# The feed-forward part's low-rank inputs moved from TensorE to a redundant weight row and to VectorE

## The chip, the cores and the metric

The kernel runs on one core of one Trainium2 chip. The core has a matrix engine (TensorE, PE in the profile, with its weight loads as PEld), three engines for elementwise work (VectorE or DVE, ScalarE or ACT, GpSimd or POOL), and SyncE (SP), which here issues most of the DMAs. Each engine works through its own queue in order; semaphores tie them together. The metric is the device time of one launch in microseconds. A smaller number is better.

## The reference

Input x has 8 sequences of 256 rows of 512. Every row is normalized, xn = (x - mean) / sqrt(var + 1e-5). Two branches start from xn:

```python
# feed-forward branch; each weight is a quarter, repeated four times, plus a rank-2 term
def linear(x, wq, A, B):
    return x @ tile(wq, (1, 4)).T + (x @ A.T @ B.T) * 0.5
h = silu(linear(xn, w1q, a1, b1)) * linear(xn, w3q, a3, b3)    # 1376 wide
g = silu(linear(h, w2q, a2, b2))                               # 512 wide
# attention branch, 128 heads: s = attention(xn), with latent q, k, v and a 64-wide rope part
out = x + s * g
```

A weight that is its quarter repeated four times needs only the sum of the four quarters of xn: xs = xn[0:128] + xn[128:256] + xn[256:384] + xn[384:512], and x @ tile(wq).T = xs @ wq.T, a contraction over 128 instead of 512. The rank-2 term has two numbers per row of x and branch (x @ a1.T, x @ a3.T) and is added on top.

The mean of each row of xn is zero, so the 128 numbers of xs sum to zero: one of them follows from the other 127. This is the redundancy that the change speaks of.

## The kernel before

The rows are taken in four blocks (`tb`) of 512. `first_phase` runs the whole feed-forward branch for all four blocks and stores its gates to DRAM; then the attention loop runs over 64 pairs of sequence and head group. Nothing is left to a planner: the order in which the code issues instructions is the order on each engine's queue. SyncE issues nearly all DMAs, in code order, and a DMA that must wait holds up those behind it.

One block on TensorE:

- `turn(tb)`: 16 transposes of the normalized x (the 128x512 tiles `xt`) into four PSUM banks; ScalarE and VectorE copy them to `act1`, feature-major. VectorE and GpSimd then add up the four quarters (`xs`, lines 429 to 431).
- `narrow(tb)`: the product `pm` of xn with `ck_sb`, which holds both low-rank inputs and the rope key; VectorE scales it into `mid` (line 446). Rows 0, 1 and 32, 33 of each half of `mid` are the low-rank numbers (already times 0.5). The rope rows go to DRAM (`krs_d`).
- `down(tb)`: the product `pp` with attention's down weights (`cs_d` in DRAM), and `sum_x`, which stores sums and differences of quarters for attention (`xs_d`), four of them computed on GpSimd (line 157).
- Six steps `u`, each for two of the eleven chunks of 128 hidden features (the last step has one). `low(tb, u)` multiplies the two low-rank numbers of each row with `b13_sb`, contraction 2, into fresh PSUM banks `px` and `py` (line 473). `main(tb, u)` adds the main product of `xs` with `w1_sb` and `w3_sb` on top (line 172, by `on_columns`, four matmuls of 32 columns side by side). ScalarE takes the silu of `px` (line 488), VectorE multiplies it with `py` into `hT` (line 490; in the last three chunks, whose 88 + 32 rows belong to different quarters, in two narrow instructions, lines 493 and 494).
- `fold` (GpSimd, lines 508 to 510) sums the quarters of `hT` into `h4`, `low_out` (line 520) makes the second layer's low-rank numbers, which line 530 and line 532 put into rows 96 and 97 of the last part of `h4`: the second layer already carries its low-rank term as two more rows of its weight.
- `gate_out`: the product `pf` over `h4`, the last silu, and four stores to `gates_d`.

The blocks overlap by hand: `norm(tb + 1)` (VectorE's statistics, GpSimd's Newton steps for the reciprocal root) stands after step 1 of block `tb`, the normalization itself (ScalarE, line 410) after step 4, `turn(tb + 1)`, `narrow` and `down` between the six steps and `gate_out(tb)`. `load_x` runs one to two blocks ahead. In the last block attention's own preparation (`between(2)` to `between(7)`: sums of rope weights, `Prepare`, `values`, `Project`) stands between the steps. `between(0)` is `set_up`: it loads and rearranges attention's up and value weights, mostly on GpSimd (lines 602 to 623), right after `narrow(0)`.

PSUM has eight banks, all from one pool. A step takes four; the tags `gate` and `hT` have two buffers each, `act1` one, `xt` six. At the start 48 transposes of the identity into a bank that nobody reads keep TensorE occupied while the first x arrives.

Of the kernel before, what the change touches and what calls it, by code (L numbers as in the profile page):

```python
# [9 lines left out]
F32 = mybir.dt.float32  # L10
# [6 lines left out]
P = 128  # L17
# [20 lines left out]
def mla_ffn_gate_kernel(  # L38
# [42 lines left out]
    cs_d = [dram.tile([P, TB], F32, name=f"cs_d{n}") for n in range(NTB)]  # L81
    krs_d = [dram.tile([R, TB], F32, name=f"kr_d{n}") for n in range(NTB)]
# [221 lines left out]
    def first_phase(between):  # L304
# [8 lines left out]
        b13_sb = fw.tile([98, NCH, P], F32, name="b13_sb")  # L313
# [4 lines left out]
        xts, xns, xnT, xsum, mids = {}, {}, {}, {}, {}  # L318
# [8 lines left out]
        def load_chunks(to, of):  # L327

            of = of.rearrange("p (q f) -> p q f", q=4)
            nc.sync.dma_start(  # L330
                out=to[:, 0:8].rearrange("p (q n) m -> p q (n m)", q=4), in_=of[:, :, 0:256]
            )
            nc.sync.dma_start(out=to[:, 8:11, 0:88], in_=of[:, 0:3, 256:344])
            nc.sync.dma_start(
                out=to[:, 8:10, 96:128],
                in_=of[:, 3, 256:320].rearrange("p (m i) -> p m i", m=2),
            )
            nc.sync.dma_start(out=to[:, 10, 96:120], in_=of[:, 3, 320:344])

        for t in (w1_sb, w3_sb, b13_sb):  # L340
            nc.gpsimd.memset(t[:, 8:11, 88:96], 0.0)
            nc.gpsimd.memset(t[:, 10, 120:128], 0.0)
# [17 lines left out]
        nc.sync.dma_start(out=wdn_sb, in_=w_down.rearrange("(c p) m -> p c m", p=P))  # L360
        for n in range(2):
            for k in range(2):
                load_chunks(
                    b13_sb[64 * n + 32 * k : 64 * n + 32 * k + 2], b13[32 * k : 32 * k + 2, :]
                )
        load_chunks(w1_sb, w1t)
        load_chunks(w3_sb, w3t)
        load_x(1)

        def norm(tb):  # L370


            mv = f2.tile([P, 4, 2], F32, tag="mv", name=f"mv_{tb}")
            for n in range(4):
                s6 = f2.tile([P, 6], F32, tag="st", name=f"st_{tb}_{n}")
                nc.vector.bn_stats(s6, xts[tb][n])
                nc.vector.bn_aggr(mv[:, n, :], s6)
# [21 lines left out]
            off = f2.tile([P, 4], F32, tag="off", name=f"off_{tb}")  # L399
            if tb:  # L400
                nc.gpsimd.tensor_mul(off, mv[:, :, 0], r)
                nc.gpsimd.tensor_scalar(off, off, -1.0, None, ALU.mult)
            return mv, r, off

        def norm_rest(tb, mv, rstd, off):
            xns[tb] = xts[tb]
            for n, xn in enumerate(xts[tb]):
                one = rstd[:, n : n + 1]
                if tb:
                    nc.scalar.activation(xn, xn, AF.Identity, bias=off[:, n : n + 1], scale=one)  # L410
                else:
                    nc.vector.tensor_scalar(xn, xn, mv[:, n, 0:1], one, ALU.subtract, ALU.mult)

        def turn(tb):
            a = f1.tile([P, KT, TB], F32, tag="act1", name=f"act1_{tb}")
            xnT[tb] = a
            for n in range(4):
# [4 lines left out]
                if n % 2 == 0:  # L422
# [4 lines left out]
            xs = f2.tile([P, TB], F32, tag="xs", name=f"xs_{tb}")  # L427
            xs2 = f1.tile([P, TB], F32, tag="tmp", name=f"xs2_{tb}")
            nc.vector.tensor_add(xs, a[:, 0, :], a[:, 1, :])
            nc.gpsimd.tensor_add(xs2, a[:, 2, :], a[:, 3, :])  # L430
            nc.vector.tensor_add(xs, xs, xs2)
            xsum[tb] = xs

        def over_xn(tb, name, weights):
            ps = bank(f"{name}_{tb}")
            for cols in (ds(0, S), ds(S, S)) if name == "pm" and tb == 0 else (ds(0, TB),):
# [6 lines left out]
        def narrow(tb):  # L443
# [3 lines left out]
            mids[tb] = mid  # L447
# [11 lines left out]
        sets, hTs, h4s, mid2ps = {}, {}, {}, {}  # L459
# [6 lines left out]
        def low(tb, u):  # L466

            sets[tb, u] = []
            for i, c in enumerate(pair(u)):
                for k in range(2):  # L470
                    ps = bank(f"p{'xy'[k]}_{tb}_{u}_{i}")
                    r = slice(64 * i + 32 * k, 64 * i + 32 * k + 2)
                    nc.tensor.matmul(  # L473
                        ps, b13_sb[r, c], mids[tb][r], start=True, stop=False, skip_group_check=True
                    )
                    sets[tb, u].append(ps)

        def main(tb, u):
            n = u // 2
# [3 lines left out]
            for i, c in enumerate(pair(u)):  # L483
                px, py = sets[tb, u][2 * i : 2 * i + 2]
                on_columns(px, w1_sb[:, c], xsum[tb], False, True)
                on_columns(py, w3_sb[:, c], xsum[tb], False, True)
                gate = f2.tile([P, TB], F32, tag="gate", name=f"gate_{tb}_{u}_{i}")
                nc.scalar.activation(gate, px, AF.Silu)
                if c < 8:
                    nc.vector.tensor_mul(h[:, c // 2, :], gate, py)  # L490
                else:
# [4 lines left out]
                    )  # L496

# [52 lines left out]
        idle = bank("idle")  # L550
        for n in range(48):
            nc.tensor.transpose(idle[:, ds(n % 4 * P, P)], ident, ident)
        norm_rest(0, *norm(0))
        turn(0)
        narrow(0)
        between(0)
        for to, of in ((a2_sb, a2), (w2_sb, w2t), (w2_sb[96:98, 2, :], b2[0:2, :])):
            nc.sync.dma_start(out=to, in_=of)
        down(0)
        for tb in range(NTB):  # L560
            more = tb + 1 < NTB
            for u in range(6):
                low(tb, u)
# [4 lines left out]
                if u == 1 and more:  # L568
                    stats = norm(tb + 1)
# [407 lines left out]
```

## Time and profile before

| | |
|---|---|
| median of three runs | 2009.84 us (2007.26 to 2011.14) |
| profiled execution | 2012.79 us, span 2011.0 us |
| granted TensorE clock, mean | 0.998 |
| busy: TensorE / VectorE / ScalarE / GpSimd | 1998.9 / 1522.8 / 1079.4 / 725.9 us |
| first product of block 0, 1, 2, 3 (line 473) | 21.73, 70.99, 122.48, 170.70 us |
| first attention score (line 688) | 238.43 us |

A line of the groups reads: line of the kernel, engine, operation, output and inputs by name, shapes, how often, then busy microseconds and the mean length of one in nanoseconds, then the idle time of the engine just before them and what ended it. A line of the timeline reads: start, length, engine, line, operation, operands, how many instructions are merged. On TensorE each float32 matmul shows as two records, and records that overlap are each shown at full length, so that the distance from start to start is the price, not the length. The chain of waits is followed back from the last instruction and says which engine each part of the span hung on.

### The profile page before, as it was taken

How to read it: one execution, taken by the hardware profiler on the slowest of the kernel's cores; microseconds unless marked ns; L12 is line 12 of the kernel's file. 1: busy time of each engine (PE TensorE's matmuls, PEld its weight loads, DVE VectorE, ACT ScalarE, POOL GpSimd, SP SyncE). 2: the span in 40 equal slices, each digit the busy share in tenths (PEclk: the TensorE clock that was granted, in tenths of full speed). 3: DMA queues.
4: the chain of work that ended last, by engine and by line, in shares of the span. 5: the costliest groups of instructions: out<-in, count | busy, mean ns of one | idle time of the engine just before them, and what ended most of it. 6: DMA issues, size and time to landing. Idle time of an engine off the chain costs nothing.

```text
span 2011.0 us, 86602 instructions
## 1 busy us (share of the span) xinstructions
PE 1998.9 (99%) x38112; PEld 1412.7 (70%) x38112; DVE 1522.8 (76%) x2601; ACT 1079.4 (54%) x2958; POOL 725.9 (36%) x1076
## 2 busy tenths in 40 slices
PE   9999999999999999999999999999999999999998
PEld 4334577777777777777777767777777767777776
DVE  4332387878788777878787877878787877888788
ACT  2222365565556554555655645565565555556654
POOL 5445545545552323233233233223323323232231
PEclk9999999999999999999999999999999999999999
DMA  5233322222223223222223233222223222222212
GB/s 169 87 113 135 113 95 84 68 87 86 86 82 123 80 91 112 91 87 78 74 86 123 66 112 105 84 81 86 81 92 102 90 93 81 86 86 72 80 55 70
DMA packets 118188, 184.78 MB, mean 92 GB/s; under 512 B 10450, under 2 KB 84082, under 8 KB 117812
## 3 DMA queue, kind: packets, MB, share of 16 engines
q1 hardware_dynamic: 117812, 179.23, 26.4%
q8 instruction: 302, 4.95, 1.0%
q14 instruction: 74, 0.61, 0.1%
HBM read 145.12 MB, written 34.08 MB: 89 GB/s over the span
## 4 chain that ended last, share of the span: by engine, by line
PE 97%; DVE 2%; issue 0%; DMA 0%; ACT 0%; POOL 0%; SPq 0%; DVEq 0%
PE q L172 39%; PE sc L688 34%; PE av L734 11%; PE po L172 2%; PE pf L172 2%; PE px L172 2%; PE py L172 2%; PE px L473 1%; PE pm L172 1%; PE qq L250 1%; PE vps L285 1%; PE pp L172 1%; DVE pt L717 1%; DVE nmx L701 0%; PE pm L520 0%; PE xpt L420 0%
## 5 line engine op out<-in xcount | busy, mean ns | idle before, releaser
L707 ACT ACTIVATE pr<-sc,nmx 128x256 f32<-128x256 f32 x2048 | 816.5, 502 | 473.8 <-DVE nmx L701 471.0
L701 DVE TENSOR_REDUCE nmx<-sc 128x2 f32<-128x512 f32 x1024 | 635.6, 683 | 291.3 <-PE sc L688 267.4
L717 DVE STREAM_TRANSPOSE pt<-pr 128x512 f32<-128x512 f32 x1024 | 635.2, 678 | 0.0
L172 PE MATMUL q<-x,ws 128*32 128x256 f32 x8192 | 488.9, 379 | 0.6 <-POOL ws L136 0.6
L688 PE MATMUL sc<-act,qr 32*128 32x256 f32 x8192 | 489.0, 374 | 0.0
L215 POOL TENSOR_TENSOR e<-e,e 128x256 f32<-128x256 f32 x128 | 93.8, 733 | 1057.5 <-ACT e L210 570.6
L688 PEld LDWEIGHTS sc<-act,qr 32*128 32x128 f32 x8192 | 421.2, 185 | 22.2 <-issue 0.2
L172 PEld LDWEIGHTS q<-x,ws 128*32 128x32 f32 x8192 | 265.7, 110 | 177.2 <-POOL ws L136 1.1
L172 PE MATMUL q<-x,w 128*32 128x256 f32 x6144 | 381.5, 381 | 0.2 <-DMA w<-in_w_rope_dram 0.2
L172 PEld LDWEIGHTS q<-x,w 128*32 128x32 f32 x6144 | 186.9, 110 | 155.0 <-ACT pr L707 35.4
L688 PE MATMUL sc<-kc,qcm 32*128 32x256 f32 x4096 | 281.2, 387 | 0.0
L734 PE MATMUL av<-pt,vpad 128*32 128x128 f32 x8192 | 236.4, 273 | 1.9 <-ACT pr L707 1.2
L734 PEld LDWEIGHTS av<-pt,vpad 128*32 128x32 f32 x8192 | 226.3, 110 | 14.5 <-issue 3.0
L688 PEld LDWEIGHTS sc<-kc,qcm 32*128 32x128 f32 x4096 | 198.4, 184 | 52.1 <-issue 40.1
L210 ACT COPY e<-q 128x256 f32<-128x256 f32 x512 | 204.1, 399 | 27.9 <-PE q L172 26.3
L754 ACT ACTIVATE acc<-av,sides_sb 128x256 f32<-128x256 f32 (+1 forms) x130 | 54.3, 470 | 245.9 <-PE av L734 245.9
L270 POOL TENSOR_TENSOR qcm<-qc,mask_sb 128x1024 f32<-128x1024 f32 x64 | 122.3, 1911 | 9.6 <-ACT qc L260 9.6
L217 POOL TENSOR_TENSOR qr<-e,e 128x256 f32<-128x256 f32 x128 | 93.7, 732 | 10.0
L216 POOL TENSOR_TENSOR e<-e,e 128x256 f32<-128x256 f32 x128 | 93.5, 731 | 10.0
L227 DVE TENSOR_TENSOR qr<-e,q 128x256 f32<-128x256 f32 x128 | 53.9, 421 | 43.4 <-POOL e L215 24.4
L300 POOL COPY vpad<-vall 32x128 f32<-32x128 f32 x256 | 74.9, 293 | 14.8 <-ACT vall L292 4.4
L490 DVE TENSOR_TENSOR hT<-gate,py 128x512 f32<-128x512 f32 x32 | 21.5, 687 | 73.9 <-PE py L172 47.4
(105 smaller groups left out, 1107.4 us busy)
## 6 DMA issues: line engine op xcount, KB each, us to landing
w<-in_w_rope_dram SPq DMA_DIRECT2D x128, 512.0 KB
ws<-sums_d SPq DMA_DIRECT2D x96, 512.0 KB
sums_d<-ws SPq DMA_DIRECT2D x32, 512.0 KB
x<-xs_d SPq DMA_DIRECT2D x28, 256.0 KB
xt<-in_x_dram SPq DMA_DIRECT2D x16, 256.0 KB
xs_d<-xt SPq DMA_DIRECT2D x16, 256.0 KB
gate_d<-gs SPq DMA_DIRECT2D x16, 256.0 KB
g<-gate_d SPq DMA_DIRECT2D x16, 256.0 KB
```

Of the source, the lines that this page charges most:

```text
L172: nc.tensor.matmul(to[tile_], w[:, tile_], x, start=start, stop=stop, skip_group_check=True)
L210: nc.scalar.copy(self.e[i], self.banks[i])
L215: nc.gpsimd.tensor_add(m6, m6, m1)
L216: nc.gpsimd.tensor_add(m7, m7, m6)
L217: nc.gpsimd.tensor_add(self.out(1, 1), self.split(m7), self.split(m5))
L270: nc.gpsimd.tensor_mul(qcm, qks[b, sg // 2][0].rearrange("p (q i) -> p q i", i=32).unsqueeze(2).to_broadcast([P, 8, 4, 32]), mask_sb[:, ds ...
L300: nc.gpsimd.tensor_copy(vpad[rows, :, :, 8 * t + 4 * (sg % 2) :][..., :4], valls[b][rows, :, sg])
L688: nc.tensor.matmul(sc[r][:, h, :], lhs.rearrange("p t i -> p (t i)"), rhs, start=(part == 0 and h == 0), stop=(part == 2), skip_group_chec ...
L701: nc.vector.tensor_reduce(nmx[:, r, :], scs[n, f][r], AX.X, ALU.max, negate=True)
L707: nc.scalar.activation(p[:, h, :], scs[n, f][r][:, h, :], AF.Exp, bias=nmxs[n, f][:, r, h : h + 1])
L717: nc.vector.transpose(pts[n, f // 2, r].rearrange("p k q i -> p q k i")[:, ds(2 * (f % 2), 2)], prs.pop((n, f, r)).rearrange("p h (k j) -> ...
L734: nc.tensor.matmul(av[32 * r : 32 * r + 32, ds(half * P, P)], vpad[:, k, r, :], pt[r][:, k].rearrange("p q i -> p (q i)"), start=(k == 0), ...
```

## The change

The low-rank input term leaves TensorE. `low` and `b13_sb` go, and `main` starts its own PSUM groups. In their place:

- Each branch has two low-rank numbers per row of x. One of them is put into row 0 of the quarter sums, in place of the number that is there, so that the main product carries it. There are now two copies of the sums, `xs0` for the first weight and `xs1` for the second, and ScalarE writes row 0 of each from `mid`. Since the true row 0 is minus the sum of the other 127, the weight's first row is subtracted from all the others, and row 0 becomes the `b13` row: `less_first` and `rest_less_first`, whose subtrahend `firsts` is made by ten matmuls of contraction 2 from `others` and `rows` and copied out by ScalarE.
- The other number is added by VectorE: `lows` holds it broadcast over all partitions (written to DRAM as `low_d` and read back with a broadcast), `bcol_sb` has the matching `b13` column per chunk, and a scalar-tensor-tensor computes `lows * bcol + px` into the gate buffer, and the same for `py`, into `hT` or back into its PSUM bank.
- The silu now works in place on the gate buffer. Of the products gate times up, six per block go to GpSimd (in block 0 three, from step 2 on), the rest stay on VectorE.
- The order changes: loads of `w1`, `w3` before `b13`; 16 idle transposes instead of 48; `norm` one block earlier from block 2 on, after `gate_out`; the normalization spread over steps 0 to 3; `turn(tb + 1)` after step 4 with all four copies on ScalarE; the quarter sums in a function of their own (`sums`); `fold` and `low_out` after steps 3 and 5; attention's raw weights loaded in `between(-1)`, their rearrangement (`set_up`) after `gate_out(0)`.

```diff
-        b13_sb = fw.tile([98, NCH, P], F32, name="b13_sb")
+        bcol_sb = fw.tile([P, 16, 2], F32, name="bcol_sb")
...
+        rows = f1.tile([P, 3 * TB], F32, tag="h4", name="rows")[:, 0:F]
+        nc.scalar.dma_start(out=rows[64:97:32], in_=b13[0:33:32, :])
+        for k, wt in enumerate((w1t, w3t)):
+            nc.scalar.dma_start(out=rows[65 + 32 * k : 66 + 32 * k], in_=wt[0:1, :])
...
+        others = f2.tile([P, TB], F32, tag="gate", name="others")[:, 0:P]
+        nc.gpsimd.memset(others[64:128], 1.0)
+        nc.gpsimd.memset(others[64:128, 0:1], 0.0)
+        for k in range(2):
+            nc.gpsimd.memset(others[64 + 32 * k : 65 + 32 * k], 0.0)
+            nc.gpsimd.memset(others[64 + 32 * k : 65 + 32 * k, 0:1], -1.0)
...
-        for n in range(2):
-            for k in range(2):
-                load_chunks(
-                    b13_sb[64 * n + 32 * k : 64 * n + 32 * k + 2], b13[32 * k : 32 * k + 2, :]
-                )
-        load_chunks(w1_sb, w1t)
-        load_chunks(w3_sb, w3t)
+        for w_sb, wt in ((w1_sb, w1t), (w3_sb, w3t)):
+            load_chunks(nc.sync, w_sb, wt)
...
+        def sums(tb):
+            a = xnT[tb]
+            xs = [f1.tile([P, TB], F32, tag=f"xs{k}", name=f"xs{k}_{tb}") for k in range(2)]
+            xs2 = f1.tile([P, TB], F32, tag="tmp", name=f"xs2_{tb}")
+            nc.vector.tensor_add(xs[0], a[:, 0, :], a[:, 1, :])
+            nc.gpsimd.tensor_add(xs2, a[:, 2, :], a[:, 3, :])
+            nc.vector.tensor_add(xs[0], xs[0], xs2)
+            nc.scalar.copy(xs[1], xs[0])
+            xsum[tb] = xs
...
+            nc.sync.dma_start(out=low_d[tb], in_=mid[1:34:32, :])
+            lows[tb] = []
+            for k in range(2):
+                t = f1.tile([P, TB], F32, tag=f"low{k}", name=f"low{k}_{tb}")
+                nc.sync.dma_start(out=t, in_=low_d[tb][k : k + 1, :].to_broadcast([P, TB]))
+                lows[tb].append(t)
+                nc.scalar.copy(xsum[tb][k][0:1], mid[32 * k : 32 * k + 1])
...
+            for i, c in enumerate(chunks):
+                px, py = (bank(f"p{'xy'[k]}_{tb}_{u}_{i}") for k in range(2))
+                on_columns(px, w1_sb[:, c], xsum[tb][0], True, True)
+                on_columns(py, w3_sb[:, c], xsum[tb][1], True, True)
+                gates.append(f2.tile([P, TB], F32, tag="gate", name=f"gate_{tb}_{u}_{i}"))
+                ups.append((py, h[:, c // 2, :] if c < 8 and (tb or u > 1) and (i == 0 or u in (0, 2)) else py))
+                nc.vector.scalar_tensor_tensor(
+                    gates[i], lows[tb][0], bcol_sb[:, place(c), 0:1], px, ALU.mult, ALU.add
+                )
+                nc.scalar.activation(gates[i], gates[i], AF.Silu)
+                nc.vector.scalar_tensor_tensor(
+                    ups[i][1], lows[tb][1], bcol_sb[:, place(c), 1:2], py, ALU.mult, ALU.add
+                )
...
+                elif up is py:
+                    nc.vector.tensor_mul(h[:, c // 2, :], gate, py)
+                else:
+                    nc.gpsimd.tensor_mul(up, gate, up)
...
+        def less_first(k, engine):
+            w_sb = (w1_sb, w3_sb)[k]
+            for c in (0, 4):
+                engine.memset(w_sb[0:1, c : c + 4], 0.0)
+                one = w_sb[:, c : c + 4]
+                engine.tensor_sub(one, one, firsts[k][:, c : c + 4])
...
         for tb in range(NTB):
             more = tb + 1 < NTB
             for u in range(6):
-                low(tb, u)
                 main(tb, u)
-                if u in (2, 4):
+                if u in (3, 5):
                     fold(tb, u // 2 - 1)
                     low_out(tb, u // 2 - 1)
-                if u == 1 and more:
-                    stats = norm(tb + 1)
+                if u == 1 and tb == 0:
+                    stats = norm(1)
+                if more:
+                    for n in range(4):
+                        if u == (n if tb else 2 + n // 2):
+                            norm_one(tb + 1, n, *stats)
                 if u == 4 and more:
-                    norm_rest(tb + 1, *stats)
+                    turn(tb + 1)
...
             if more:
-                turn(tb + 1)
+                sums(tb + 1)
+                narrow(tb + 1)
                 low_out(tb, 2)
-                narrow(tb + 1)
                 down(tb + 1)
             else:
                 low_out(tb, 2)
             gate_out(tb)
+            if tb == 0:
+                between(0)
+            if tb + 2 < NTB:
+                stats = norm(tb + 2)
```

## The prediction

> **What bounds the kernel now.** I read the page first (engines and the chain that ended last), then the groups of the first 270 us with shapes apart, then TensorE's timeline and the stages as windows, last the clock.
>
> ```profile
> PE 1998.9 (99%) x38112; PEld 1412.7 (70%) x38112; DVE 1522.8 (76%) x2601; ACT 1079.4 (54%) x2958; POOL 725.9 (36%) x1076
> ...
> PE 97%; DVE 2%; issue 0%; DMA 0%; ACT 0%; POOL 0%; SPq 0%; DVEq 0%
> ```
>
> TensorE is 97% of the chain. A TensorE instruction that goes away shortens the run by its length, as long as what feeds and empties TensorE keeps up. That second half is what must be worked out.
>
> ```profile
> L473 PE MATMUL py<-mid,b_sb 2*128 2x512 f32 x88 | 28.4, 640 | 0.0
> ...
> L490 DVE TENSOR_TENSOR hT<-gate,py 128x512 f32<-128x512 f32 x32 | 21.5, 687 | 73.9 <-PE py L172 47.4 <-ACT gate L488 26.4
> ...
> L508 POOL TENSOR_TENSOR h<-hT 128x512 f32<-128x512 f32 x8 | 10.5, 1308 | 0.1
> ...
> L532 DVE SCALAR_TENSOR_TENSOR h<-pm,h 32x512 f32<-32x512 f32 x12 | 8.3, 691 | 1.4 <-ACT h L530 1.0
> ...
> L431 DVE TENSOR_TENSOR xs<-xs,xs 128x512 f32<-128x512 f32 x4 | 6.0, 1490 | 11.0 <-POOL xs L430 11.0
> ...
> L446 DVE TENSOR_SCALAR mid<-pm,cks_sb 128x512 f32<-128x512 f32 x4 | 3.0, 752 | 0.4 <-PE pm L172 0.3
> ```
>
> Line 473 is the low-rank input product, and VectorE's product at line 490 spends its time waiting. One step `u` of the timeline, block 2:
>
> ```profile
> 127.12 0.69 PE L473 MATMUL px<-mid,b_sb 2*128 2x512 f32 x1
> ...
> 128.19 1.07 PE L172 MATMUL px<-xs,w_sb 128*32 128x512 f32 x8
> ...
> 131.76 0.69 PE L473 MATMUL px<-mid,b_sb 2*128 2x512 f32 x1
> ```
>
> Start to start the step is 4.64 us; the four products in it follow each other at 0.86 (128.19, 129.07, 129.93, 130.79) and make 3.43, so `low` takes 1.21. The stages (blocks 0, 1, 2, then 3):
>
> ```profile
> 23.00:71.00 48.00, 47.63 (x413) 15.39 (x406) 19.56 (x34) 13.68 (x22) 34.54 (x67) 1.00 0.41 138
> 71.00:122.50 51.50, 51.38 (x428) 16.45 (x424) 19.49 (x33) 13.90 (x23) 21.89 (x29) 0.97 0.31 106
> 122.50:170.70 48.20, 48.08 (x424) 15.52 (x421) 19.59 (x33) 14.01 (x23) 27.57 (x37) 1.00 0.31 102
> 170.70:240.00 69.30, 69.30 (x980) 31.13 (x980) 14.98 (x25) 20.77 (x44) 35.18 (x43) 1.00 0.33 111
> ```
>
> Columns: stretch, length, busy of TensorE, its weight loads, VectorE, ScalarE, GpSimd, granted clock, DMA share, GB/s. VectorE has 19.5 of 48 us to do, room that the change fills. Block 1 is 3.3 us longer than block 2: ScalarE's gate stores waited up to 6 us for their buffer (line 547's transfers), TensorE ran dry for PSUM, and the clock fell:
>
> ```profile
> 79.00:80.00 1.00, 1.00 (x12) 0.72 0.70 266
> 80.00:81.00 1.00, 1.00 (x8) 0.50 0.61 221
> ```
>
> **Removed from TensorE.** 24 steps `low` by 1.21 us: 29.0 us, all on the path. Without it a block that keeps up is 22 products by 0.86 (18.9), `low_out` 2.8, `turn` 1.9, `pm` 3.43, `pp` 3.43, `pf` 10.44: 40.9 us against 48.2.
>
> **Added to VectorE.** Per block 22 scalar-tensor-tensor, each reading a broadcast row in SBUF, a column and a PSUM bank. No row shows this form. Line 532 (691, no column) bounds it below and line 431 above (mean 1490, 1754 in the three runs beside a reading GpSimd, 692 in the one without; two SBUF operands). I take 0.75, from line 446 (752), which has the column and the PSUM read. It also stands for the half that writes back into PSUM, of which there is no row. Products left on VectorE from block 1: two plus six of the narrow chunks, 8 by 0.69. Sum 16.5 + 5.5 = 22.0 us in the window in which TensorE does main, `low_out` and `turn`, 22.5. It fits by half a microsecond, with `pm`'s 3.43 as reserve before `low_out` 2 needs the last product.
>
> **Two gate buffers, GpSimd's products.** Six products per block go to GpSimd, 1.3 each (line 508). A gate buffer is free only after its product, so the next step's first VectorE operation waits for GpSimd: 0.75 + 0.75 + 1.31 = 2.8 us of a step's 3.43. Steady state holds. It breaks where GpSimd is busy with other things.
>
> **Block 0.** Three things are late here. (a) `lows` go through DRAM: `mid` ends at 19.2, the write and two 256 KB reads follow. The first x tile, on idle queues, took 2.8 us from issue (0.73 to 3.54); line 123's rope weights took 4.1 (195.35 to 199.43). Two such trips: 6 to 8.5 us; I take 6.0, the queues being near empty once the weights are in, so 25.2. TensorE does not stop; it has two steps of banks. (b) VectorE then does 8 operations and 4 products, 8.75 us (33.95), and only then `norm(1)`, 3.8 us (32.40 to 36.2 on the trace): 37.75. (c) GpSimd's 14 small steps, 4.0 us (41.51 to 45.39): 41.8. Two queues stand behind that. On ScalarE the normalizations of x for block 1 wait for it, and the later gates wait behind them. On GpSimd the two products of step 2 wait for it (first one done at 43.1), and they hold both gate buffers, so VectorE starts step 3 only at 43.1 and ends it, its product included, at 46.8 (four by 0.75 and 0.69). In step 4 VectorE frees the second gate's bank at 49.05, ScalarE's gate ends at 49.65, and `turn(1)`'s four copies, now all on ScalarE and behind that gate, end at 52.0 (four by 0.59). Its first two narrow products free the bank that step 5 lacks at 51.2 (46.8 + 3.0 + 1.4). From there TensorE is the bound again: step 5's second half, `low_out` 1, `pm`, `low_out` 2, `pp` and `pf` (0.86, 0.86, 3.43, 1.07, 3.43, 10.44) end at 71.3, against 71.0 now. So block 0 gives its 7.25 us back: +0.3. Bounds: trip of 2.8 us less, -3; of 8.5, +3, and 3 more if the clock falls (below).
>
> **Start-up.** 32 idle transposes go (4.6 us of the 6.9); ten products that copy the first rows come in: four 512 wide at 0.86 and six short, 4.6 us, and their ten copies on ScalarE, 4 us (0.59 for 512). TensorE has 8.25 to 11.17 and the freed time, ScalarE is idle to 12.32. Cover gone (rows landing after 7 us): up to 4 later. Three new DMAs stand on ScalarE's queue. On SP, 16 small `b13` loads go, two weight parts and six small loads come; the weights move from 12.4 to about 4.2, `x` for block 1 with them. Subtractions: GpSimd two by 1.28 and two fills by 0.53 after 17.44, first half ready at 19.3; VectorE's two after `mid`, 0.69 to 1.75 each, first half by 21.5; both before use at 21.7 and 22.6. The remaining chunks are due 17 us later. ScalarE's row copies (0.59 each) end at 20.4. Sum 0, bounds -1 and +4.
>
> **Block 1.** It loses the old 3.3 us only in part: SP waits out `low_d`'s write and issues two reads, some 2.8 us ahead of `kr_d`, `cs_d`, seven `xs_d` and the gate stores. By the same positions the first gate store is issued at about 71.5, as now, but TensorE needs the third bank 5.15 us after `pf` either way, so up to 1 us. `set_up` (27.48 to 36.4 on the trace, 8.9 us of GpSimd) now stands after `gate_out(0)`, with `norm(2)` behind it: GpSimd is free 6.5 us into block 1, its products are 4 us late, and through the gates VectorE is late by 3.5; TensorE's banks take most, 2 reach step 5. 40.9 + 2 + 0.6 = 43.5: -8.0 (bounds -11 and -4).
>
> **Blocks 2 and 3.** Block 2: 7.25 less 0.5 for the gates: -6.7. In block 3 attention's projections lie between the steps, VectorE has time, and GpSimd's two `sum_w` (5.9 us) stand before step 1's product: 2 us late, covered by values and Project. -6.7. Bounds -7.25 and -3 each. Attention, from 240 us on, is unchanged.
>
> Sum: 0 + 0.3 - 8.0 - 6.7 - 6.7 = -21.1. The profiled execution is 2012.79 (span 2011.0 and 1.8 around it), 2.95 above the median of 2009.84; from the median: **1988.7**.
>
> **A rule against it.** After the poor stretch 76 to 79 the trace shows half clock for some 3 us; block 0 will have TensorE idle about 43 to 47. The Trainium skill, "TensorE: Matmul & The Clock Gate", Part 1, has the clock halved after an idle window of about 3.4 us and whole after as much work. By that rule block 0 would come out some 2 us later, total about -19; the row at 80.00 agrees with a drop of that length. I kept 3 us in block 0's bound.
>
> **Rivals.** (1) Everything keeps up: `lows` early, no idle: 29 us and block 1's 3.3: -27 to -32, 1980. For it: GpSimd and ScalarE are under 60%. Against: the chain in block 0. (2) Half: VectorE at 0.85 with latencies between the engines costs 22 by 0.1 plus a step per block, some 3 us in four blocks, -10, 2000. For it: margin of 0.5 us in 22.5. (3) **Slower**, by one mechanism: the new operation, with row and column both in SBUF, is held up by GpSimd as line 431 is. At 1.75 VectorE has 22 us more per block, less 3.4 of reserve, less 7.25: +11.4, in three blocks +34, 2044. It decides at (7.25 + 3.4)/22 = 0.48 more, 1.23 us each. Against: lines 493 and 494 took 0.68 with GpSimd's line 508 running at 96.9; line 446 with its column 0.751 at 112.2, beside line 157. The Trainium skill, "SBUF — State Buffer", section "Who interferes with whom", says that a VectorE instruction with two SBUF inputs contends with a reading GpSimd, one with at most one does not; counting the column as an input would make it this rival. Line 446's row shows no such cost for a column, so the chance stays small. (4) Nothing is left: every term at its bad bound, +4 at the start, +6 in block 0, -4, -3 and -3 after it, sums to 0: within 0.2%, about 2010.
>
> **Chances.** Forecast (-16 to -26) 0.50; (1) 0.12; (2) (-5 to -16) 0.22; (4) 0.05; (3) 0.11. A fifth of a per cent, 4 us, is about what can be told from no change. Faster 0.84, same 0.05, slower 0.11. The forecast with (2) and most of (1): 1981 to 2004; the forecast's own 1984 to 1994.
>
> **What would show it.** Line 473 gone; blocks 1 and 2 near 43.5 and 41.5 us; block 0 about 48 with VectorE waiting for `lows` near 25, a gap in TensorE at 43 to 47 and `norm(1)` ahead of it. The new operation near 0.75 and the same with GpSimd busy. Wrong if it is over 1.2, if TensorE waits in every block on gates, or if block 0 ends well before 70.

## The result and the profile after

| | before | after |
|---|---|---|
| median | 2010.03 us (2007.26 to 2011.14, 4 runs) | 1996.68 us (1995.26 to 1999.53, 4 runs) |
| profiled execution, span | 2012.79, 2011.0 | 1999.53, 1997.7 |
| first low-rank or main product of block 0, 1, 2, 3 | 21.73, 70.99, 122.48, 170.70 | 26.48, 72.74, 115.85, 158.70 |
| first attention score | 238.43 | 225.04 |

The ratio is 0.9935, 95% interval 0.9921 to 0.9949: 13.35 us less by the medians, where 21.1 were forecast. Both profiled executions lie 2.8 to 2.9 above the median of their kernel, so the stages of the two can be set against each other.

The page of the changed kernel, engines and chain:

```profile
PE 1978.8 (99%) x38021; PEld 1408.9 (71%) x38021; DVE 1568.8 (79%) x2666; ACT 1093.7 (55%) x2987; POOL 761.4 (38%) x1114
...
PE 91%; POOL 4%; DVE 3%; issue 2%; DMA 0%; ACT 0%; POOLq 0%; DVEq 0%; ACTq 0%
```

TensorE lost 20.1 us of busy time, and its share of the chain fell from 97% to 91%. GpSimd's new products and its folds (lines 549 and 561 to 563) have come into the chain, where before it had nothing. The stages of blocks 0 to 3 as windows (stretch, length, busy of TensorE, its weight loads, VectorE, ScalarE, GpSimd, clock, DMA share, GB/s), each from the first main product to the next:

```profile
26.48:72.74 46.26, 41.96 (x409) 14.23 (x412) 34.57 (x61) 18.00 (x29) 36.91 (x66) 1.00 0.44 149
72.74:115.85 43.11, 41.89 (x412) 14.76 (x408) 29.95 (x49) 17.03 (x28) 33.17 (x48) 1.00 0.33 117
115.85:158.70 42.85, 41.38 (x412) 14.63 (x408) 26.57 (x38) 17.02 (x28) 29.39 (x35) 1.00 0.39 133
158.70:225.04 66.34, 62.49 (x909) 27.11 (x901) 26.24 (x41) 19.35 (x42) 48.09 (x57) 0.97 0.38 133
```

Against before (start to start 49.26, 51.49, 48.22, 67.73) the blocks are shorter by 3.0, 8.4, 5.4 and 1.4. The first product comes 4.75 later. That makes 13.4, all of it ahead of 225.04: attention took 1772.6 us before and 1772.7 after. The step `u` of block 2, which was 4.64 long, in TensorE's timeline:

```profile
123.62 1.04 PE L173 MATMUL px<-xs,w_sb 128*32 128x512 f32 x8
...
127.05 1.04 PE L173 MATMUL px<-xs,w_sb 128*32 128x512 f32 x8
```

It is 3.43 now, as worked out. The groups of the new operation (lines 532 and 536) and of GpSimd's products (line 549), which the prediction priced by lines 446 and 508 of before; idle time and its releaser stand at the end:

```profile
L532 DVE SCALAR_TENSOR_TENSOR gate<-low,bcol_sb,px 128x512 f32<-128x512 f32 x44 | 32.8, 744 | 34.8 <-POOL hT L549 24.9 <-PE px L173 6.2 <-DMA low<-low_d 2.4
...
L536 DVE SCALAR_TENSOR_TENSOR py<-low,bcol_sb,py 128x512 f32<-128x512 f32 x23 | 17.3, 750 | 0.2
L536 DVE SCALAR_TENSOR_TENSOR hT<-low,bcol_sb,py 128x512 f32<-128x512 f32 x21 | 15.6, 743 | 0.8
L549 POOL TENSOR_TENSOR hT<-gate,hT 128x512 f32<-128x512 f32 x21 | 26.8, 1286 | 23.4 <-ACT gate L535 23.3
```

The new operation costs what was taken for it, 0.74 to 0.75, in both forms. VectorE waited 24.9 us before it for GpSimd's products. What TensorE waited for between 22 and 232 us, longest first (us in total, times, longest one); before, the same view had a single wait of 0.4:

```profile
PE q L173 <- ACT e L211: 2.7, 1, 2.7
PE py L173 <- ACT gs L599: 1.8, 2, 1.1
PE py L173 <- DVE gate L532: 1.7, 1, 1.7
PE px L173 <- DVE gate L532: 1.6, 3, 0.6
PE pm L573 <- DVE gate L532: 0.8, 1, 0.8
PE xpt L458 <- DVE hT L547: 0.8, 1, 0.8
```

Three places carry the difference to the forecast. The first is the start, TensorE's timeline:

```profile
1.35 3.68 PE L606 MATMUL idle<-ident 128*128 128x128 f32 x16 [1.35 <-POOL ident masks.py:199]
5.07 9.77 PE L624 MATMUL first<-rows,others 2*128 2x512 f32 x20
14.77 3.67 PE L458 MATMUL xpt<-ident,xt 128*128 128x128 f32 x16
18.37 4.57 PE L173 MATMUL pm<-act,ck_sb 128*32 128x256 f32 x64
```

The ten first-row matmuls (twenty records) fill TensorE for 9.77 us, and the transposes of x, ready near 10.7, stand behind them until 14.77 (11.17 before).

The second is block 0. VectorE's timeline, and under it GpSimd's:

```profile
28.99 0.75 DVE L532 SCALAR_TENSOR_TENSOR gate<-low,bcol_sb,px 128x512 f32<-128x512 f32 x1 [2.38 <-DMA low<-low_d]
...
36.65 0.70 DVE L407 BATCH_NORM_STATS2 st<-xt 128x6 f32<-128x512 f32 x1
...
45.82 0.75 DVE L532 SCALAR_TENSOR_TENSOR gate<-low,bcol_sb,px 128x512 f32<-128x512 f32 x1 [2.63 <-POOL hT L549]
```

```profile
44.31 0.23 POOL L441 TENSOR_SCALAR off<-off 128x4 f32<-128x4 f32 x1
44.51 2.51 POOL L549 TENSOR_TENSOR hT<-gate,hT 128x512 f32<-128x512 f32 x2
```

The chain `lows`, steps 0 and 1, `norm(1)`, GpSimd's small steps, step 2's products, step 3 is there link by link. TensorE stands still for 1.72 us until 46.62.

The third is block 3. GpSimd, VectorE, ScalarE and TensorE, each from its timeline:

```profile
175.14 1.90 POOL L271 TENSOR_TENSOR qcm<-qc,mask_sb 128x1024 f32<-128x1024 f32 x1
177.00 1.28 POOL L549 TENSOR_TENSOR hT<-gate,hT 128x512 f32<-128x512 f32 x1
```
```profile
178.31 0.75 DVE L532 SCALAR_TENSOR_TENSOR gate<-low,bcol_sb,px 128x512 f32<-128x512 f32 x1 [6.65 <-POOL hT L549]
```
```profile
180.47 0.63 ACT L535 ACTIVATE gate<-gate 128x512 f32<-128x512 f32 x1 [0.75 <-DVE gate L532]
181.01 1.18 ACT L211 COPY e<-q 128x256 f32<-128x256 f32 x4
```
```profile
181.41 3.24 PE L173 MATMUL q<-x,w 128*32 128x256 f32 x32 [2.74 <-ACT e L211]
```

GpSimd works off two `sum_w` and the spread of `qcm` before step 1's product, VectorE waits 6.65 us for the gate buffer, step 2's silu comes late on ScalarE, and `Project`'s copies (line 211), which stand behind it in ScalarE's queue, hold up TensorE for 2.74. The granted clock during and behind that wait, as windows of the same columns as above:

```profile
180.00:182.00 2.00, 0.59 (x8) 0.36 (x12) 1.04 (x2) 1.53 (x5) 1.98 (x2) 0.67 0.00 0
182.00:184.00 2.00, 2.00 (x28) 0.85 (x24) 0.00 (x0) 0.56 (x2) 1.87 (x3) 0.50 0.04 8
```

### The profile page after: what moved, and what is told of

The parts are those of the page before. It is cut to its first block, busy times and chain, and to the rows that moved or that the text cites. A ratio compares the mean times of both kernels' runs of the same rounds, so it can differ in the third digit from the quotient of the medians.

```text
span 1997.7 us, 86602 instructions
## 1 busy us (share of the span) xinstructions
PE 1978.8 (99%) x38021; PEld 1408.9 (71%) x38021; DVE 1568.8 (79%) x2666; ACT 1093.7 (55%) x2987; POOL 761.4 (38%) x1114
## 4 chain that ended last, share of the span: by engine, by line
PE 91%; POOL 4%; DVE 3%; issue 2%; DMA 0%; ACT 0%; POOLq 0%; DVEq 0%; ACTq 0%
PE q L173 39%; PE sc L804 34%; PE av L850 11%; PE po L173 3%; POOL hT L549 1%; PE pf L173 1%; PE qq L251 1%; DVE pt L833 1%; POOL h4b L562 1%; POOL h L561 1%; PE vps L286 1%; PE first L624 0%; DVE nmx L817 0%; POOL h L563 0%; DVE hT L536 0%
## 5 line engine op out<-in xcount | busy, mean ns | idle before, releaser
L876 POOL TENSOR_TENSOR acc<-acc,acc 128x256 f32<-128x256 f32 (+1 forms) x66 | 48.7, 759 | 39.1 <-ACT acc L870 39.1
```

## The experiments

All stages come from the profiled execution of each kernel; the medians decide on the total. "Start" is the first main product.

| kernel | median us | ratio to before, 95% | start | blocks 0, 1, 2, 3 | attention |
|---|---|---|---|---|---|
| changed kernel | 1996.68 | 0.9935 (0.9921 to 0.9949) | 26.48 | 46.26, 43.11, 42.85, 66.34 | 1772.7 |
| e1_pairs | 1997.69 | 0.9935 (0.9920 to 0.9950) | 25.73 | 46.15, 43.17, 42.76, 65.42 | 1773.0 |
| e2_warm48 | 1997.61 | 0.9936 (0.9921 to 0.9951) | 25.45 | 47.33, 42.91, 42.68, 63.96 | 1773.6 |
| e3_block3 | 1993.84 | 0.9917 (0.9902 to 0.9931) | 26.62 | 46.29, 43.16, 43.00, 62.01 | 1771.5 |
| e4_store_act | 2002.16 | 0.9963 (0.9949 to 0.9978) | 26.20 | 46.38, 42.87, 43.08, 66.04 | 1775.5 |
| e5_norm | 1995.52 | 0.9928 (0.9911 to 0.9945) | 26.62 | 43.56, 43.22, 42.61, 65.06 | 1772.1 |
| e6_broadcast | 2000.37 | 0.9949 (0.9934 to 0.9964) | 24.37 | 48.08, 43.57, 42.76, 66.95 | 1772.6 |
| e7_no_second | 1983.79 (one run) | | 24.66 | 42.31, 41.05, 40.68, 60.75 | 1772.7 |
| e8_three | 1992.88 | 0.9912 (0.9898 to 0.9927) | 25.53 | 45.74, 43.29, 42.70, 62.18 | 1771.8 |
| e9_two | 1992.48 | 0.9908 (0.9893 to 0.9922) | 26.36 | 44.12, 42.93, 42.82, 62.77 | 1773.3 |
| e10_start | 1988.87 | 0.9890 (0.9873 to 0.9906) | 21.44 | 45.29, 43.38, 42.86, 62.01 | 1771.7 |

Each group of kernels was timed beside the kernel before, whose median was 2010.03 for the changed kernel, 2010.29 for e1 to e4, 2010.55 for e5 to e8 and 2010.95 for e9 and e10. So a difference of a microsecond between two medians of this table says little.

### The start: the first-row matmuls

**e1_pairs.** The theory: ten matmuls one after another are too long, and if those of the two weights alternate, two can run side by side.

```diff
-        for k in range(2):
...
-            for i, (one, two) in enumerate(by_chunks(to, rows[of])):
...
-            for one, ps in copies:
-                nc.scalar.copy(one, ps)
+            parts.append([(k, i, of, one, two) for i, (one, two) in enumerate(by_chunks(to, rows[of]))])
...
+        for pairs in zip(*parts):
+            copies = []
+            for k, i, of, one, two in pairs:
...
+            for one, ps in copies:
+                nc.scalar.copy(one, ps)
```

> The ten first-row matmuls are issued in pairs, one of each weight in turn (row groups 64 and 96), so that two can run side by side; nothing else changes. Theory (the start-up lost 4.75 us because ten contraction-2 matmuls ran one after another at half rate, 5.07 to 14.77, before the transposes that wait behind them): they end near 10.0, the transposes start near 10.7, when their input is ready, and the first main product moves from 26.48 to about 22.5; total 4 us less than the changed kernel's 1996.7. Rival (the half clock is what costs, not the number in a row): the transposes and pm still run at half rate and the first product comes no more than 1 us earlier.

The start moved by 0.75 and the total not at all. TensorE's timeline of this kernel:

```profile
4.96 1.41 PE L627 MATMUL first<-rows,others 2*128 2x512 f32 x2
8.31 6.04 PE L627 MATMUL first<-rows,others 2*128 2x512 f32 x18 [1.95 <-POOL cks_sb L374]
14.29 3.67 PE L458 MATMUL xpt<-ident,xt 128*128 128x128 f32 x16
```

A better order did not cure it. The second weight's first matmul begins only at 8.31. Its row comes by the third load on ScalarE's queue, issued at 3.94; that this row was the last thing it waited for is inferred, since line 374, which the trace names as releaser, writes nothing that these matmuls read. The remaining eighteen records then take 6.04 us, so they end at 14.35, half a microsecond earlier than in the changed kernel.

**e2_warm48.** Is it the rate of TensorE? The 48 idle transposes of before come back.

```diff
-        warm(16)
+        warm(48)
```

> 48 idle transposes again instead of 16, all else as changed. Theory (contraction-2 matmuls do not bring the clock up and do not hold it): the first-row matmuls start at 8.25 and take between 4.9 and 9.8 us, so the first main product comes at 26 to 29, no gain or up to 3 us lost. Rival (16 transposes were too few to bring the clock up, and that alone is the loss): the matmuls take 4.9 us, transposes and pm run at full rate, the first product comes near 22.5 and the total falls by 4 us.

```profile
1.35 6.79 PE L606 MATMUL idle<-ident 128*128 128x128 f32 x48 [1.35 <-POOL ident masks.py:199]
8.07 7.05 PE L624 MATMUL first<-rows,others 2*128 2x512 f32 x20
15.05 3.27 PE L458 MATMUL xpt<-ident,xt 128*128 128x128 f32 x16
18.26 3.66 PE L173 MATMUL pm<-act,ck_sb 128*32 128x256 f32 x64
```

The first-row matmuls are shorter (7.05 for 9.77) but begin 3 us later; `pm` is down from 4.57 to 3.66. So the rate is part of it, but the start gains 1.0, block 0 loses 1.1, and the total stays. The theory's mechanism is there in the clock: in windows of 2 us it reads 1.00 up to 10, 0.74 from 10 to 12, 0.50 from 12 to 16, 0.56 from 16 to 18 and 1.00 again from 18. From 1.35 on TensorE was occupied without a pause; the clock fell while it ran the first-row matmuls and came back towards the end of the transposes of x.

**e6_broadcast.** No first-row matmuls at all: the first rows come by broadcast DMAs, and the bias row is copied over a zeroed row 0.

```diff
+            load_chunks(nc.sync, to, wt[0:1, :].to_broadcast([P, F]))
...
-                nc.tensor.matmul(
-                    ps, others[of], two, start=True, stop=True, skip_group_check=True
-                )
...
+            nc.gpsimd.memset(firsts[k][0:1], 0.0)
```

> The subtrahend of the first rows is loaded by broadcast DMAs behind w1 and w3 on SyncE's queue (1.4 MB more), and row 0 is copied from b13 instead of zeroed; the ten contraction-2 matmuls and their ten copies go. Theory (those matmuls, waiting for their rows until 8.3 and running in front of the transposes, cost the start-up 4.75 us): transposes start near 10.8 as before the change, the first main product moves from 26.5 to about 22, total -4.5. Rival (the added transfers cost as much): x for block 1 and lows land later, the first product comes at 22 but block 0 is 3 us longer or more.

A miss: 2000.37, 3.7 above the changed kernel (1999.52 to 2000.65 against 1995.26 to 1999.53). The transposes began at 10.03, 4.7 us earlier, but the first main product at 24.37. GpSimd's timeline shows why:

```profile
17.02 1.26 POOL L609 MEMSET first<- 1x1408 f32 x1 [7.89 <-DMA first<-in_w1t_dram]
19.29 1.26 POOL L609 MEMSET first<- 1x1408 f32 x1 [1.01 <-DMA chunk_rows<-in_b_dram]
20.53 1.26 POOL L469 TENSOR_TENSOR xs<-act 128x512 f32<-128x512 f32 x1
```

My two zeroings wait for the loads and stand in front of GpSimd's half of the sum of x (19.33 in the changed kernel). On VectorE `mid` stands behind that sum (22.82, after 23.02 in the changed kernel), so `lows` come hardly earlier, and the main product waits 2.91 us for GpSimd's subtraction. The start was given back in GpSimd's queue. e10 below takes this one obstacle away.

### Block 3

**e3_block3.** The theory: GpSimd's products, behind `sum_w` and the spread, make step 2 late on VectorE, then on ScalarE, then `Project`. In block 3 alone all products stay on VectorE.

```diff
-                ups.append((py, h[:, c // 2, :] if c < 8 and (tb or u > 1) and (i == 0 or u in (0, 2)) else py))
+                ups.append((py, h[:, c // 2, :] if c < 8 and (tb or u > 1) and tb < NTB - 1 and (i == 0 or u in (0, 2)) else py))
```

> In block 3 alone all products gate times up stay on VectorE, so no gate buffer waits for GpSimd there. Theory (block 3 lost 5 us because step 1's product stands behind two sum_w and a spread on GpSimd, holds the gate buffers, and through ScalarE's queue holds Project's copies): block 3 falls from 66.3 to about 62.5, the 2.7 us wait of Project's second half goes, blocks 0 to 2 stay; total -4. Rival (the late gate stores at the start of the block are the cause): no more than 1 us, the wait for the copies stays.

Block 3 fell from 66.34 to 62.01. ScalarE's first copy and TensorE's product of the lines above, now:

```profile
176.41 0.37 ACT L211 COPY e<-q 128x256 f32<-128x256 f32 x1 [0.25 <-PE q L173]
```
```profile
178.72 1.98 PE L173 MATMUL q<-x,w 128*32 128x256 f32 x32
```

No wait, and 1.98 us for the 32 records that took 3.24. The median is 2.84 below the changed kernel's, not 4. Block 3 measured 63.96 to 66.95 in the five other kernels that keep its products on GpSimd (e1, e2, e4, e5, e6), so the profile of the changed kernel, its slowest run, shows it near its worst. All five have the wait for the copies (2.72 to 3.80). Behind it the granted clock stayed at 1.00 in e1, e2 and e5, with a block 3 of 64.81 on average, and fell in e4, e6 and the changed kernel, with 66.44. By these averages about 1.6 of the 4.3 us belong to the clock, which falls in some executions only, and 2.8 to the wait.

**e4_store_act.** The rival: it is the gate stores, late on SP's queue, that delay ScalarE's last silus of the block before (7 us of its wait at 164.86 ended with line 600's transfer).

```diff
-                nc.sync.dma_start(out=gates_d[4 * tb + n], in_=gs)
+                nc.scalar.dma_start(out=gates_d[4 * tb + n], in_=gs)
```

> The four gate stores of each block are issued from ScalarE's queue instead of SyncE's, where they stood behind the low_d, kr_d, cs_d and seven xs_d transfers. Theory: the third silu of gate_out comes 4 to 5 us earlier in each block; blocks 1 and 2 gain 0.7 each from the PSUM bank, block 1 up to 1 more because its gates and GpSimd's first products are no longer late, block 3 gains 1.3 and keeps the 2.7 us wait for Project's copies behind GpSimd's sum_w; total -3 to -4. Rival (the late stores alone made block 3's chain late): block 3 falls to 61 and the wait for the copies goes; total -6 to -7. Second rival (transfers are limited by bandwidth, not by the queue): no change.

Refuted. In block 1 the third silu came at 74.86 instead of 79.30 and the block's first gate at 79.21 instead of 80.54, yet the block changed by 0.24. GpSimd is busy with `set_up` and the small steps of `norm(2)` until 81.03 in the changed kernel and until 80.84 here, and its products start behind them. So that wait was covered. Block 3 kept a wait for `Project`'s copies (3.80) and measured 66.04. And a new cost appeared at the end, on ScalarE:

```profile
229.18 0.60 ACT L599 ACTIVATE gs<-pf 128x512 f32<-128x512 f32 x1 [0.99 <-DMA gate_d<-gs]
229.80 0.33 ACTq L600 DMA_DIRECT2D gate_d<-gs  x1
230.16 1.28 ACT L698 ACT_TABLE_LOAD   x1 [0.39 <-ACT gs L599]
```

In the changed kernel the last silu starts at 226.61 and attention's first exponential at 229.48; here at 232.41. Attention is 2.8 us longer. The median is 5.5 higher; the other 2.7 are in no stage of these profiles (the changed kernel's profiled execution is 2.85 above its median, this one 0.1 below) and stay open.

### Block 0

**e5_norm.** The theory: `norm(1)`, issued after step 1, is what delays step 3. It is issued ahead of step 0, into the 2.38 us in which VectorE waits for `lows`.

```diff
+        stats = norm(1)
         for tb in range(NTB):
...
-                if u == 1 and tb == 0:
-                    stats = norm(1)
```

> norm(1) stands before step 0 of block 0 instead of after step 1, where its statistics held VectorE from 36.65 to 40.47 and GpSimd's small steps behind them held step 2's products until 44.51. Theory (this chain made block 0 5.4 us longer than its 40.9 us of TensorE work): VectorE does the statistics while it waits for lows (26.6 to 29.0), the first new operation starts up to 1.5 us later, block 0 falls from 46.3 to 42.5 to 43.5, total -3. Rival (the late lows alone set block 0): no change or 1.5 us longer.

Block 0 fell to 43.56. VectorE's step 0 now starts later, at 32.33, and step 3 earlier, at 42.85 for 45.82:

```profile
42.85 0.75 DVE L532 SCALAR_TENSOR_TENSOR gate<-low,bcol_sb,px 128x512 f32<-128x512 f32 x1 [0.16 <-POOL hT L549]
```

The stage gain is 2.7. The median fell by only 1.16, within the spread of the runs (1993.5 to 1998.29 against 1995.26 to 1999.53): the mechanism is shown by the stage, a gain in the total by this kernel alone is not.

### What the second low-rank number costs

**e7_no_second.** This kernel leaves out part of the computation: the second low-rank number of each branch is not added. ScalarE takes the silu straight from PSUM, and all products stay on VectorE.

```diff
-                nc.vector.scalar_tensor_tensor(
-                    gates[i], lows[tb][0], bcol_sb[:, place(c), 0:1], px, ALU.mult, ALU.add
-                )
-                nc.scalar.activation(gates[i], gates[i], AF.Silu)
+                nc.scalar.activation(gates[i], px, AF.Silu)
```

> Leaves out the second low-rank number of each branch: no scalar-tensor-tensor, ScalarE's silu reads PSUM and all products stay on VectorE; the start-up is as changed. It shows what TensorE alone needs once the contraction-2 product is gone. Theory: blocks 1 and 2 come to 41 to 42 us, block 3 to 61 to 62, block 0 to 42 to 43; so VectorE's new work costs 1 to 2 us in a middle block and 4 to 5 in blocks 0 and 3. Rival (the new work is hidden and something else, such as the late gate stores, holds the blocks): no block shortens by more than 1 us.

Blocks 1 and 2 are 41.05 and 40.68: the 40.9 that I had added up from TensorE's rows is TensorE's own price. Against it the full kernel is longer by 3.95, 2.06, 2.17 and 5.59. So VectorE's operations, with the buffers and GpSimd products around them, cost 13.8 us of path, and most of it lies in blocks 0 and 3.

### Together

**e8_three.** e6, e3 and e5 in one kernel (their diffs above).

> The broadcast start-up, norm(1) before step 0, and block 3's products on VectorE together. Theory (three separate places): -4.5, -3 and -4.3 add up, total near 1985, 0.6% below the changed kernel and 1.2% below the kernel before. Rival (the savings overlap, or the next wait takes over, the gate stores first): no more than 7 us below the changed kernel, 1990.

1992.88, the rival's side: e6's zeroing still puts GpSimd's sum at 21.70 and `mid` at 23.98.

**e9_two.** e3 and e5 alone, on the changed kernel's own start.

> Block 3 with all its products on VectorE, and norm(1) ahead of block 0's first step, both on the changed kernel's own start-up. If the two delays are independent, the stages are those of the two single runs: main starts near 26.5, blocks of 43.5, 43.2, 42.7 and 62.0, attention from 218.0 instead of 225.04: about 1989.7 us. Rival: the profiles of the single runs flatter them (their medians were 2.8 and 1.2 below the changed kernel's, not 4 each), then the sum of the medians, 1992.7.

1992.48, near the rival's 1992.7: the sum of the two medians' gains (2.84 and 1.16) fits better than that of the single profiles. The four runs go from 1989.83 to 1994.90, so the total alone can't settle it, nor set e9 apart from e3.

**e10_start.** e8 with one thing changed: nothing is zeroed, and the bias row is copied over row 0 after the subtraction.

```diff
-        for k in range(2):
-            nc.gpsimd.memset(firsts[k][0:1], 0.0)
...
-                own_row(k, engine, (c // 4,))
                 one = w_sb[:, c : c + 4]
                 engine.tensor_sub(one, one, firsts[k][:, c : c + 4])
+                own_row(k, engine, (c // 4,))
```

> As e8_three, but the bias rows are copied over row 0 after the subtraction instead of zeroing the first rows before it, so nothing that waits for a load stands ahead of GpSimd's sum of x. Theory: block 0 hangs on the chain sum of x, mid, lows. GpSimd's sum then comes near 14.5 instead of 21.70, mid near 18.5 instead of 23.98, the first new operation near 24.5, TensorE's first low-rank main matmul near 22 instead of 25.53 and block 0 near 43.5 instead of 45.74: 5 to 6 us less than e8_three's 1992.9, about 1987. Rival: another resource sets the start (VectorE's row copies and subtractions, or the weights' loads), then the start of block 0's first step on VectorE stays near 28 and the total stays above 1990.

1988.87, 22 us below before and 7.8 below the changed kernel, faster than every other kernel here that does the whole computation. GpSimd, VectorE, TensorE:

```profile
15.19 1.78 POOL L469 TENSOR_TENSOR xs<-act 128x512 f32<-128x512 f32 x1 [5.39 <-DVE act L461]
```
```profile
18.69 0.74 DVE L486 TENSOR_SCALAR mid<-pm,cks_sb 128x512 f32<-128x512 f32 x1
19.35 1.67 DVE L619 TENSOR_TENSOR w_sb<-w_sb,first 128x512 f32<-128x512 f32 x1
...
28.85 0.73 DVE L530 SCALAR_TENSOR_TENSOR gate<-low,bcol_sb,px 128x512 f32<-128x512 f32 x1
```
```profile
10.69 3.61 PE L456 MATMUL xpt<-ident,xt 128*128 128x128 f32 x16 [5.67 <-DVE xt L448]
14.24 3.66 PE L173 MATMUL pm<-act,ck_sb 128*32 128x256 f32 x64
```

`mid` came at 18.69 and the first main product at 21.44, as the theory had them (18.5, 22). One edit, which takes the zeroing out of GpSimd's queue and on both engines puts the row copies behind the subtractions, moved the start by 4.1 us against e8, and the total by 4.0. The rest of the theory missed, and there the rival was right: the new operation starts at 28.85, not 24.5, because VectorE itself is full from 18.69 on (`mid`, subtractions, row copies, `norm(1)`), and block 0 is 45.29, not 43.5. So in this kernel VectorE, not the trip of `lows`, holds back block 0's first step. Moving the second weight's subtraction elsewhere wasn't tried.

## Why the prediction was right, and where not

The direction and the mechanism held: TensorE's time fell out, VectorE took the new operation at its forecast price, and the delays came in the chains named. The gain was 13.35 of 21.1. That lies in the wide range (1981 to 2004), but outside the forecast's own (1984 to 1994, chance 0.50); it lies in the range given to rival 2 (chance 0.22). Two misses partly cancel in it: the start and block 0. Term by term, from the profiled executions:

- **Removed, 29.0 us.** Right. The step is 3.43, and a block that keeps up is 40.7 to 41.1 (e7) for the 40.9 added up.
- **The new operation, 0.75.** Right, 0.743 to 0.750 in all three groups. Rival 3 fell: two of them at 168.14 and 168.81, while GpSimd's products ran (166.83 to 169.36), took 0.75 and 0.74. A subtraction with two SBUF operands did stretch in e10: 1.67 at 19.35, beside GpSimd's subtraction of the same width. The same line took 0.70 at 22.50, with GpSimd at narrower subtractions. The Trainium skill, "SBUF — State Buffer", section "Who interferes with whom", has VectorE contend with a reading GpSimd when two inputs come from SBUF. The trace agrees at 19.35; at 22.50 VectorE lost nothing, and why is open. The products at 168.14 show that the column operand does not count as such an input.
- **Start-up, forecast 0 with bounds -1 and +4: it was +4.75.** The failed step is "four 512 wide at 0.86 and six short, 4.6 us": they took 9.77, and the transposes of x stand behind them on TensorE. The 0.86 is a price of the steady state, and TensorE isn't at that rate there. The risk that I had named, rows landing after 7, did not cost this kernel anything: the twenty records run from 5.07 to 14.77 without a wait, and only e1's order ran into it. The row that could have told it is the start of before itself: 16 transposes of x took 3.61 there at 11.17, against 1.97 for sixteen at 49.76. e10, which has no first-row matmuls and nothing that waits for a load ahead of GpSimd's sum of x, starts at 21.44, as early as before (21.73).
- **Block 0, forecast +0.3: it was -3.0.** The two belong together. I had worked out the block's end as a time on the trace, 71.3; it came at 72.74. `lows` came at 28.99 for 25.2 (`mid` ended 4.6 late, the trip took 5.2 for 6.0), step 3 at 45.82 for 43.1, the end 1.4 late. The chain from `mid` sets the end, and TensorE's later start only ate the time that it would have spent waiting: in e1, e2 and e6, which start 0.75, 1.0 and 2.1 earlier, block 0 ends at 71.88, 72.78 and 72.45. Start and block 0 together: +1.75 for +0.3. e5 and e10 confirm two links, `norm(1)` and `mid`; the gap in TensorE forecast for 43 to 47 is there, but 1.72 us.
- **A rule against it.** The granted clock stayed at 1.00 through that gap, so the 3 us kept for it in the bound weren't needed in block 0. It fell in block 3 instead, during a wait of 2.74 that no step of the prediction had: the windows read 0.67 from 180 to 182 and 0.50 from 182 to 184, and the 32 records after the wait took 3.24 for e3's 1.98. The Trainium skill, "TensorE: Matmul & The Clock Gate", Part 1, asks for an idle window of about 3.4 us. Here the stretch 178 to 182, with 1.26 us of work in it, was enough; in e1, e2 and e5 a wait of the same length (2.73 to 2.76) left the clock at 1.00.
- **Block 1, forecast -8.0: it was -8.4.** Right, with one cause less than I gave: ScalarE's wait for the gate stores lasted 7.4 us and was covered by GpSimd's `set_up` and `norm(2)`, as e4 showed.
- **Block 2, forecast -6.7: it was -5.4.** "0.5 for the gates" was 2.2 by e7: mis-sized. TensorE waited 0.66 for the gate stores and 0.38 for a gate. The prediction's sign of being wrong, that TensorE waits on gates in every block, is there in small: up to 1.72 in block 0, 0.60 in block 1, 0.38 in block 2.
- **Block 3, forecast -6.7: it was -1.4.** This is the largest miss, 5.3 of the 7.7 us. The step reads "2 us late, covered by values and Project". `Project` isn't a cover: its copies are on ScalarE's queue behind the silu that was late, so lateness on VectorE becomes a TensorE wait through a third engine. I had counted `sum_w`, but not the spread of `qcm` (1.90), and the delay was 6.65. e3 shows it: without GpSimd's products the wait is gone, and the block takes 62.01, 5.7 less than before. By the averages given there, about 1.6 of the miss are the clock's, which fell in this execution.

Sums: start +4.75, blocks -3.0, -8.4, -5.4, -1.4, together -13.4 in the span. Rival 2 (half, -10) has the nearer total, but that is luck: VectorE at 0.85 per operation, its cause, did not occur. Rival 1 fell with the 13.8 us that VectorE's part costs. The loss against the forecast came at the start and in block 3, by what stood ahead in a queue.

## What to carry to other kernels

When work moves to an engine that has time, look for what already stands in that engine's queue at that moment, and then follow the late result into the next engine's queue: work that seems to cover a delay does so only if none of it is queued behind the late instruction. Price TensorE's first instructions by rows from the kernel's own first microseconds, not from its steady state. And set a single-profile gain against the spread of that stage over other kernels that leave it alone, before adding gains up.

## What the runs showed of the hardware

- Matmuls of contraction 2 did not bring TensorE to its rate, nor hold it there. In e2, occupied without a pause from 1.35, the granted clock fell to 0.50 during the first-row matmuls and came back towards the end of the transposes of x (windows of e2 above). In the changed kernel it was occupied from 1.35 without a pause, and the transposes at 14.77 still took 0.23 us each. The windows read 1.00 there, but that is no measurement: the trace's first entry of the clock is at 20.3 us, and nothing before it says what was granted. In e10, idle for 5.67 us until 10.69, `pm` ran whole (3.66) from 14.24. Reading each `pm` over 3.66 as begun at half rate (twice the excess), the whole rate came 3.6 us or less after the first transpose of x in e10, 4.7 in e6 and 5.4 in the changed kernel, but there 19 us after TensorE became occupied. The Trainium skill, "TensorE: Matmul & The Clock Gate", Part 1, has the clock restored by some 3.4 us of sustained activity, which fits the first three numbers roughly and the last not, unless a two-row matmul isn't activity; e2's clock points that way. That the height of the operand decides was not isolated.
- The same ten first-row matmuls took 9.77 us in the changed kernel and 7.85 in e7, with the same code ahead of them: the start of this kernel is not the same from run to run. In e7 the clock reads 1.00 until 8 us, 0.52 from 8 to 10 and 0.50 until 18, so a part of them ran at the whole rate there.
- A 4 KB write to DRAM and two 256 KB broadcast reads took 5.2 us from `mid`'s end to the first operation that used them.
